# Second attention of a two-layer block by units of four heads, with projections and head outputs kept in DRAM

## The chip, the cores and the metric

The kernel runs on one core of a Trainium2 chip. A core has a matrix engine (PE, TensorE), a vector engine (DVE), an activation engine (ACT), a general engine (POOL) and a sync engine (SP) that only issues transfers; each takes its own instructions in order, and they wait for one another by semaphores. PE writes its results to PSUM, of which this program lays out eight banks of 512 float32 per partition; DVE and ACT read them from there. The metric is the device time of one execution in microseconds, the median over several runs.

## The reference, cut to what matters

Input x is 4 batches of 2048 rows of 256. Everything is float32.

```python
x = L0_attn_x
xn = _layernorm(x)
s = _L0_attn_ref(xn, Wqkv, Wout)          # 16 heads of 16; segments of 512 rows, every 8th row a key
g = _silu(_L0_ffn_ref(xn, ...))           # x rounded to fp8, 256 x 256 product, bias
x = x + s * g
xn = _layernorm(x)
s = _L1_attn_ref(xn, ...)                 # causal attention, 16 heads of 16, rotary q and k
g = _silu(_L1_ffn_ref(xn, ...))           # mixture of 8 experts, 2 per row, capacity 2048 rows each
x = x + s * g

# second attention
q, k, v = projections with bias; q, k = _apply_rope(q, k)
att = softmax(where(causal, q k^T / 4, -inf)); y = att v; return y wo^T + bo
# second feed-forward: logits -> softmax -> top 2 -> place of each row in its expert's 2048 slots
h = relu(disp w1 + b1); out = h w2 + b2   # 256 -> 1024 -> 256 per expert
y = gate-weighted sum of each row's two results
```

The second attention subtracts each row's true maximum, so every score is computed twice: once for the maxima, once for the exponentials.

## The kernel before, in words

*First layer.* Sixteen segments of 512 rows go through a software pipeline that is written as a plan: `segment(g)` enters its steps under a step number (`at(t0 - 20, load)` and so on), and one loop emits them by number. PSUM is split into two pairs for scores (`sc_tile`, two banks each) and four single banks (`mm_tile`). Most SBUF tiles have two buffers. The normalized result x1n goes to `xn_d` in DRAM, x1 to `x1_d`.

*Routing.* After the first layer, softmax of the logits, the two best experts, running counts by doubling (`scan`), and a table `source` of which row sits in which expert slot; the table is built by 128 one-hot pairs that one accumulating matmul (L542) adds up, with `at_row` from DVE (L538). Nothing else runs beside it.

*Second layer.* PSUM is now three pairs (`pair_tile`, L683's scores) and two single banks (`one_tile`). A ring of five blocks holds q, k and v of 512 rows for all 16 heads in SBUF. For each batch there are two stages:

- `maxima(b)`: for each block of 512 queries, each tile of 128 of them and each group of four heads, the scores against each block of 512 keys (L683, four matmuls on the four row groups of the array) into two pairs; DVE takes maxima of a pair (L720). On the diagonal ACT copies the 128 x 128 part (L723), POOL masks it (L731), DVE takes its maximum (L740), and L725 takes the part left of it. The negated maxima are turned (`spread`) and written by DMA into a spare row of q, so that the second scores come out with the maximum subtracted.
- `attend(b)`: for each block, group and tile of 128 keys, scores again, exponential on ACT (L826), on the diagonal a POOL mask (L831), and two items later (`LAG = 2`) the product with v (L846), which sums in one single bank; then `heads_out` and `out_rows` turn, divide and project.

`project` (L619 turns x1n, L626 q and k, L635 v, L652 to L657 the rotation, L666 and L671 the turn into the ring) and `experts` (L915 turns the gathered rows, L926 first product, L930 relu on ACT, L941 second product, L947 bias on DVE) are generators; a yield names a rough cost. `along` walks the main stage and lets side generators catch up with their share: in maxima two experts, in attend the next batch's projections. Beside the last attend runs `finish`, which gathers each row's two expert results and writes the output. The order on PE, DVE, ACT and POOL is that of emission.

Of the kernel before, what the change touches and what calls it, by code (L numbers as in the profile page):

```python
# [18 lines left out]
P = 128  # L19
# [24 lines left out]
def d2_kernel(ctx: ExitStack, tc: tile.TileContext, t: dict):  # L44
# [6 lines left out]
    first = ExitStack()  # L51
    ps_sc = first.enter_context(tc.tile_pool(name="ps_sc", bufs=2, space=PSUM))
    ps_mm = first.enter_context(tc.tile_pool(name="ps_mm", bufs=4, space=PSUM))

    def sc_tile():
        return ps_sc.tile([P, 2, 512], F32, tag="sc", name="sc")

    def mm_tile():
        return ps_mm.tile([P, 512], F32, tag="mm", name="mm")
# [6 lines left out]
    xn_d = dram.tile([B * M + 1, D], F32, tag="xn_d", name="xn_d")  # L66
    s_d = dram.tile([B * M, D], F32, tag="s_d", name="s_d")
# [7 lines left out]
    def rows(d, n):  # L75
# [11 lines left out]
    early = ExitStack()  # L87
    logits = early.enter_context(tc.tile_pool(name="early", bufs=1)).tile(
        [P, NT, E], F32, tag="logits", name="logits"
    )  # L90
# [28 lines left out]
    def transpose2(out, in_):  # L119

        tp = mm_tile()
        for c in range(2):
            nc.tensor.transpose(tp[:, c * P : (c + 1) * P], in_[:, c * P : (c + 1) * P], ident)
        nc.scalar.copy(out, tp[:, : 2 * P].rearrange("p (c t) -> p c t", c=2))

    def silu(pool, zh):

        th = pool.tile([P, D], F32, tag="se", name="se")
        nc.scalar.activation(th, zh, AF.Tanh)
        nc.vector.scalar_tensor_tensor(zh, th, 1.0, zh, ALU.add, ALU.mult)  # L130


    with ExitStack() as l0:
        w0 = l0.enter_context(tc.tile_pool(name="w0", bufs=1))
        p2 = l0.enter_context(tc.tile_pool(name="l0p2", bufs=2))
        small = l0.enter_context(tc.tile_pool(name="l0small", bufs=4))
# [27 lines left out]
        for i in range(3):  # L164
            v_ = w0.tile([P, 8, 2, HD + 1], F32, tag=f"vbd{i}", name=f"vbd{i}")
            nc.vector.tensor_copy(v_[:, :, :, HD], bc(dmask[:, None, :], [P, 8, 2]))
            vbds.append(v_)
# [7 lines left out]
        def at(step, f, *args):  # L175
            plan.setdefault(step, []).append((f, args))

        def segment(g):
# [3 lines left out]
            def load():  # L182
                v["x"] = x = p2.tile([P, SPT, D], F32, tag="x", name="x", bufs=6)
                nc.sync.dma_start(out=x, in_=rows(x_d, g))
# [7 lines left out]
            def norm(tag):  # L192
                v[tag] = xn = p2.tile([P, SPT, D], F32, tag=tag, name=tag)
# [5 lines left out]
            def turn_x(c):  # L199
                if c == 0:  # L200
                    v["xnT"] = p2.tile([P, 2, SEG], F32, tag="xnT", name="xnT")

                    v["xdil"] = p2.tile([P, 2, 2, KN], F32, tag="xdil", name="xdil")
                tp = mm_tile()
                for a in range(SPT):
                    nc.tensor.transpose(
                        tp[:, a * P : (a + 1) * P], v["xn"][:, a, c * P : (c + 1) * P], ident
                    )
                nc.scalar.copy(v["xnT"][:, c, :], tp)
                for u in range(2):  # L210
                    nc.gpsimd.tensor_copy(v["xdil"][:, c, u, :], v["xnT"][:, c, ::DIL])

            def to_fp8(half):


                if half == 0:
                    v["xq"] = xq = p2.tile([P, 2, SEG], F32, tag="xq", name="xq", bufs=3)
# [4 lines left out]
                mag = p2.tile([P, 2, SEG], F32, tag="mag", name="mag")  # L222
# [7 lines left out]
            def q_proj(ec):  # L230
                if ec == 0:
                    v["qT"] = p2.tile([P, 2, SEG], F32, tag="qT", name="qT")
                pq = mm_tile()
                for c in range(2):
                    nc.tensor.matmul(  # L235
                        pq, lhsT=wqkv[:, c, ec * P : (ec + 1) * P], rhs=v["xnT"][:, c, :],
                        start=(c == 0), stop=(c == 1),
                    )
                nc.scalar.mul(v["qT"][:, ec, :], pq, SCALE)

            def k_proj():

                pk = mm_tile()
                for ec in range(2):
                    for c in range(2):
                        nc.tensor.matmul(
                            pk[:, ec * KN : (ec + 1) * KN],
# [3 lines left out]
                v["kbd"] = kbd = p2.tile([P, 2, 2, KN], F32, tag="kbd", name="kbd")  # L251
                for ec in range(2):
                    nc.vector.tensor_tensor(
                        kbd[:, ec, :, :],
                        bc(pk[:, None, ec * KN : (ec + 1) * KN], [P, 2, KN]),
                        bc(hmask[:, :, None], [P, 2, KN]), ALU.mult,
                    )

            def v_proj():
                pv = mm_tile()  # L260
                for c in range(2):
                    nc.tensor.matmul(
                        pv[:, :D], lhsT=v["xdil"][:, c, :, :].rearrange("p u k -> p (u k)"),
                        rhs=wqkv[:, c, 2 * D : 3 * D], start=(c == 0), stop=(c == 1),
                    )
                for u in range(2):
                    nc.vector.tensor_scalar(  # L267
                        vbds[g % 3][:, :, u, 0:HD],
                        pv[:, :D].rearrange("p (j u d) -> p j u d", u=2, d=HD)[:, :, u, :],
# [3 lines left out]
            def scores0(ec):  # L273

                scs = [sc_tile(), sc_tile()]
                for pr in (2, 3, 0, 1):
                    r0 = 32 * pr
# [275 lines left out]

    early.close()
    first.close()

# [573 lines left out]
```

## Time and profile before

| | |
|---|---|
| time, median of 3 runs | 4508.95 us (4506.05 to 4519.44) |
| the profiled execution: its time, its span | 4471.85 us, 4470.1 us |
| busy PE; DVE; ACT; POOL | 4090.9; 2447.8; 1664.1; 851.3 us |
| mean granted PE clock | 0.932 |
| instructions | 57281 |
| written to and read from HBM | 48.24 and 86.03 MB |

A matmul in float32 shows as two records, so "x8" in a timeline is four matmuls. Matmuls are pipelined and their ends are modelled: distances from start to start tell more than busy time. In the group list a line names the engine, the operation, output and inputs, shape, count, busy time and mean, and then the idle time before these instructions with what ended it.

### The profile page before, as it was taken

To read this page: it belongs to the slowest core of one execution; us is meant where nothing else is said; L and a number is where in the kernel's file an instruction comes from. 1 tells how busy PE (TensorE), PEld (TensorE's weight loads), DVE (VectorE), ACT (ScalarE), POOL (GpSimd) and SP (SyncE) were. 2 spreads that over 40 slices of the span, in tenths; PEclk is the share of its full clock that TensorE was granted. 3 is DMA by queue.
4 is the path that set the end of the run, shared out by engine and by line. 5 is a ranking of instruction groups with operands and counts; after the bars stand their busy time and mean duration, and the time that the engine had idled before them with its cause. 6 is when DMAs were issued, how large, how long until landed. Compare 5 with 4: busy or idle time off the path is not lost.

```text
span 4470.1 us, 57281 instructions
## 1 busy us (share of the span) xinstructions
PE 4090.9 (92%) x23560; PEld 1930.8 (43%) x23560; DVE 2447.8 (55%) x3622; ACT 1664.1 (37%) x2548; POOL 851.3 (19%) x1067
## 2 busy tenths in 40 slices
PE   7898966789999998899999998999999989999998
PEld 4666654344443333444433334444333344443333
DVE  7777777667761122777812226777312257775334
ACT  2333310111116664222156652211566522114775
POOL 3333323101100012111100012110000121112444
PEclk8888777699999998899999998999999989999999
DMA  2111000000100001001000001010000010102422
GB/s 77 43 43 43 29 33 25 10 15 24 38 20 6 10 6 41 20 20 39 15 10 6 10 14 46 16 40 18 6 10 6 15 36 20 39 20 74 128 94 75
DMA packets 111240, 138.48 MB, mean 31 GB/s; under 512 B 11393, under 2 KB 99842, under 8 KB 110978
## 3 DMA queue, kind: packets, MB, share of 16 engines
q1 hardware_dynamic: 95922, 98.22, 6.7%
q0 software_dynamic: 12288, 33.57, 2.4%
q8 instruction: 185, 3.03, 0.3%
q10 hardware_dynamic: 2768, 3.02, 0.2%
q14 instruction: 77, 0.63, 0.0%
HBM read 86.03 MB, written 48.24 MB: 30 GB/s over the span
## 4 chain that ended last, share of the span: by engine, by line
PE 79%; DVE 15%; issue 2%; DMA 1%; ACT 1%; POOL 1%; POOLq 0%; ACTq 0%; SPq 0%; DVEq 0%
PE sp L683 29%; PE so L846 11%; PE so L926 10%; PE so L941 9%; DVE mp L720 4%; PE so L626 3%; PE mm L300 2%; PE so L666 2%; PE mm L323 1%; PE so L635 1%; PE so L787 1%; PE sc L278 1%; DVE at_row L538 1%; PE mm L328 1%; PE mm L235 1%
## 5 line engine op out<-in xcount | busy, mean ns | idle before, releaser
L826 ACT ACTIVATE pt<-sp 128x1024 f32<-128x1024 f32 (+3 forms) x1280 | 1076.8, 893 | 577.2 <-PE sp L683 541.6
L720 DVE TENSOR_REDUCE mp<-sp 128x2 f32<-128x1024 f32 x768 | 904.5, 1220 | 317.7 <-PE sp L683 314.9
L683 PE MATMUL sp<-kT,qT 32*128 32x512 f32 (+3 forms) x5120 | 785.1, 615 | 63.9 <-DVE mp L725 25.9
L683 PE MATMUL sp<-qT,kT 32*128 32x512 f32 (+3 forms) x5120 | 783.4, 583 | 13.6 <-ACT pt L826 13.5
L846 PE MATMUL so<-pt,va 128*32 128x512 f32 (+3 forms) x5120 | 604.6, 545 | 10.9 <-POOL pt L831 10.9
L723 ACT COPY dg<-sp 128x256 f32<-128x256 f32 x512 | 165.3, 375 | 962.6 <-PE sp L683 899.1
L926 PE MATMUL so<-xTe,w 128*128 128x512 f32 x1024 | 515.9, 628 | 4.3 <-ACT xTe L918 2.0
L941 PE MATMUL so<-w,hT 128*128 128x256 f32 x2048 | 506.6, 392 | 0.3 <-DVE ot L947 0.3
L731 POOL TENSOR_SCALAR_AFFINE_SELECT dg<-dg 128x512 f32<-128x512 f32 x256 | 163.2, 640 | 1578.7 <-ACT dg L723 1578.6
L683 PEld LDWEIGHTS sp<-kT,qT 32*128 32x128 f32 x5120 | 270.6, 197 | 444.6 <-issue 146.0
L683 PEld LDWEIGHTS sp<-qT,kT 32*128 32x128 f32 x5120 | 282.9, 184 | 407.6 <-issue 254.0
L941 PEld LDWEIGHTS so<-w,hT 128*128 128x128 f32 x2048 | 374.0, 191 | 193.2 <-issue 143.5
L831 POOL TENSOR_SCALAR_AFFINE_SELECT pt<-pt 128x512 f32<-128x512 f32 x256 | 171.7, 672 | 1310.4 <-PE sp L683 677.1
L930 ACT ACTIVATE hT<-so,b 128x512 f32<-128x512 f32 x256 | 176.0, 687 | 572.5 <-PE so L926 572.5
L725 DVE TENSOR_REDUCE mp<-sp 128x2 f32<-128x256 f32 (+2 forms) x384 | 247.5, 687 | 145.2 <-ACT dg L723 144.2
L926 PEld LDWEIGHTS so<-xTe,w 128*128 128x128 f32 x1024 | 178.1, 193 | 283.1 <-issue 199.6
L846 PEld LDWEIGHTS so<-pt,va 128*32 128x32 f32 x5120 | 101.5, 108 | 418.9 <-issue 345.0
L852 DVE COPY avs<-so 128x512 f32<-128x512 f32 x64 | 44.2, 691 | 360.7 <-PE so L846 360.7
L740 DVE TENSOR_REDUCE mp<-dg 128x8 f32<-128x1024 f32 x128 | 155.0, 1211 | 31.5 <-POOL dg L731 31.5
L626 PE MATMUL so<-wqk,xT 128*128 128x512 f32 x256 | 139.9, 672 | 23.8 <-DVE xT L622 9.5
L294 ACT ACTIVATE w<-w 128x1024 f32<-128x1024 f32 x64 | 67.7, 1057 | 241.4 <-DVE w L290 241.4
L300 PE MATMUL mm<-vbd,w 128*128 128x34 f32 x1024 | 128.7, 283 | 21.5 <-DVE vbd L267 21.5
(165 smaller groups left out, 3514.9 us busy)
## 6 DMA issues: line engine op xcount, KB each, us to landing
w<-in_w_dram SPq DMA_DIRECT2D x16, 1024.0 KB, 6.3
eout<-ot SPq DMA_DIRECT2D x32, 512.0 KB, 2.9
x<-in_x_dram SPq DMA_DIRECT2D x16, 512.0 KB, 5.9
x_d<-x SPq DMA_DIRECT2D x16, 512.0 KB, 2.9
xn_d<-x1n SPq DMA_DIRECT2D x16, 512.0 KB, 3.2
xn<-xn_d SPq DMA_DIRECT2D x16, 512.0 KB
fx<-x_d SPq DMA_DIRECT2D x16, 512.0 KB, 5.5
out_dram<-fz SPq DMA_DIRECT2D x16, 512.0 KB, 4.1
```

The source lines that it names most:

```text
L300: nc.tensor.matmul(av[:, j * 34 : (j + 1) * 34], lhsT=v["w", j // 2][:, j % 2, a * P : (a + 1) * P], rhs=vbds[g % 3][:, j, :, :].rearrange ...
L626: nc.tensor.matmul(pqk, lhsT=xT[:, c, :], rhs=wqk[:, c, :], start=(c == 0), stop=(c == 1))
L683: nc.tensor.matmul(pairs[j // 2][:, j % 2, :w], lhsT=lhsT[r0 : r0 + 32], rhs=rhs[r0 : r0 + 32], start=True, stop=True,)
L720: nc.vector.tensor_reduce(mp[:, h0 : h0 + 2, kc], sp, AX.X, ALU.max)
L723: nc.scalar.copy(dg[:, d0 : d0 + 2, :], sp[:, :, r * P : w])
L725: nc.vector.tensor_reduce(mp[:, h0 : h0 + 2, qb + 1], sp[:, :, : r * P], AX.X, ALU.max)
L826: nc.scalar.activation(pt[:, 2 * p : 2 * p + 2, c0:], sp[:, :, : SEG - c0], AF.Exp, scale=SCALE)
L831: nc.gpsimd.affine_select(out=pt[:, :, c0 : c0 + P], in_=pt[:, :, c0 : c0 + P], compare_op=ALU.is_ge, fill=0.0, base=0, pattern=[[0, 4], [ ...
L846: nc.tensor.matmul(av[32 * j : 32 * j + 32, c0:], lhsT=va[:, kt % 4, h0 : h0 + 32], rhs=pt[:, j, c0:], start=(kt == 0), stop=last,)
L926: nc.tensor.matmul(ph, lhsT=w1[:, c, hc * P : (hc + 1) * P], rhs=xT[:, c, :], start=(c == 0), stop=(c == 1),)
L930: nc.scalar.activation(hT[:, hc, :], ph, AF.Relu, bias=b1[:, hc : hc + 1])
L941: nc.tensor.matmul(po[:, u * D : (u + 1) * D], lhsT=hT[:, hc, a * P : (a + 1) * P], rhs=w2[:, hc, :], start=(hc == 0), stop=(hc == 7),)
```

## The change

PSUM has one layout for the whole program: three pairs (`ps_s`), one bank for the sums of attend (`ps_v`), one bank for everything else (`ps_m`, `mm_tile`). The first layer's scores, x, q, value and output tiles use the pairs too, in two halves of a segment instead of four quarters; most of its SBUF tiles have one buffer.

The first layer also stores x1n turned (`xT_ds`). `project` loads that instead of turning, and writes q, k and v to DRAM by batch, q and k by groups of four heads. A unit is one group of four heads of one batch, 16 units in all; `load_unit` brings its q, k and v into one of two sets of SBUF tiles. `attention` runs the first unit's maxima alone and then, for each unit, attend of it beside maxima of the next, one item of each per step, maxima three steps behind (`LEAD`). The values follow their scores by one item instead of two. Head outputs go to DRAM (`y_ds`), and `out_project` loads them back by blocks of 512 rows.

Batch 0's projections run beside the first layer, routing beside the first unit's maxima, the experts after it in all steps up to 13.7 units, `finish` from there. Projection and output pieces are placed between a step's scores and its values, expert pieces after its maxima. Routing's one accumulating matmul became 16 groups of eight, each added on DVE. The second expert product of 512 columns in two halves became one bank of 256 columns per 128 rows.

```diff
-    ps_sc = first.enter_context(tc.tile_pool(name="ps_sc", bufs=2, space=PSUM))
-    ps_mm = first.enter_context(tc.tile_pool(name="ps_mm", bufs=4, space=PSUM))
+    ps_s = ctx.enter_context(tc.tile_pool(name="ps_s", bufs=3, space=PSUM))
+    ps_v = ctx.enter_context(tc.tile_pool(name="ps_v", bufs=1, space=PSUM))
+    ps_m = ctx.enter_context(tc.tile_pool(name="ps_m", bufs=1, space=PSUM))
...
-    ps_s = ctx.enter_context(tc.tile_pool(name="ps_s", bufs=3, space=PSUM))
-    ps_m = ctx.enter_context(tc.tile_pool(name="ps_m", bufs=2, space=PSUM))
...
+    xT_ds = [dram.tile([2, P, M], F32, tag=f"xT_d{b}", name=f"xT_d{b}") for b in range(B)]
+    q_ds = [dram.tile([4, P, M], F32, tag=f"q_d{b}", name=f"q_d{b}") for b in range(B)]
+    k_ds = [dram.tile([4, P, M], F32, tag=f"k_d{b}", name=f"k_d{b}") for b in range(B)]
+    v_ds = [dram.tile([M, H * (HD + 1)], F32, tag=f"v_d{b}", name=f"v_d{b}") for b in range(B)]
+    y_ds = [dram.tile([M, D], F32, tag=f"y_d{b}", name=f"y_d{b}") for b in range(B)]
...
+    def project():
...
+                xT = pp.tile([P, 2, SEG], F32, tag="pxT", name="pxT")
+                nc.sync.dma_start(
+                    out=xT, in_=xT_ds[b][:, :, i * SEG : (i + 1) * SEG].rearrange("c p t -> p c t")
+                )
...
+                            st = pp.tile([P, 4, P], F32, tag="st", name="st", bufs=3)
+                            nc.vector.tensor_copy(st, tp.rearrange("p (g t) -> p g t", g=4))
+                            nc.sync.dma_start(
+                                out=dst[:, :, t0 + u * P : t0 + (u + 1) * P].rearrange(
+                                    "g p t -> p g t"
+                                ),
+                                in_=st,
+                            )
+                            yield 0.55
...
+    def load_unit(n):
+        b, g = n // 4, n % 4
+        held[n] = sets[(sets.index(held[n - 1]) + 1) % len(sets) if n else 0]
+        qT, kT, va = held[n]
+        nc.sync.dma_start(out=qT, in_=q_ds[b][g])
+        nc.sync.dma_start(out=kT, in_=k_ds[b][g])
+        nc.sync.dma_start(
+            out=va[:, :, :VW],
+            in_=v_ds[b][:, g * VW : (g + 1) * VW].rearrange("(i p) c -> p i c", p=P),
+        )
...
+    def attend(n):
...
+                pt = at.tile([P, 4, SEG], F32, tag="pt", name="pt")
+                pairs = scores(
+                    SEG - c0, kT[:, kt * P : (kt + 1) * P], qT[:, qb * SEG + c0 : (qb + 1) * SEG]
+                )
+                for p, sp in enumerate(pairs):
+                    nc.scalar.activation(
+                        pt[:, 2 * p : 2 * p + 2, c0:], sp[:, :, : SEG - c0], AF.Exp, scale=SCALE
+                    )
...
+            yield 1
+            if step:
+                qb, kt = items[step - 1]
+                ppt, c0 = last_pt
+                if kt == 0:
+                    av = ps_v.tile([P, SEG], F32, tag="av", name="av")
...
+    def attention():
+        NU = 4 * B
+        LEAD = 3
...
+        yield from start(0)
+        for _ in maxima(0):
+            yield MX_T, 1
+            turn()
+        for n in range(NU):
+            two = len(sets) == 2 and n + 1 < NU
+            if two:
+                yield from start(n + 1)
+            a = attend(n)
+            m = maxima(n + 1) if two else iter(())
+            a_on, step = True, 0
+            while True:
+                if a_on:
+                    a_on = next(a, None) is not None
+                    if a_on:
+                        yield S_T, 0
+                        next(a)
+                m_on = step < LEAD or next(m, None) is not None
+                if not (a_on or (two and m_on)):
+                    break
+                yield (AV_T if a_on else 0.0) + (MX_T if two and step >= LEAD else 0.0), 1
+                turn()
+                step += 1
...
+    def out_project(pool, done):
...
+            y = pool.tile([P, SPT, D], F32, tag="oy", name="oy")
+            nc.sync.dma_start(out=y, in_=rows(y_ds[b], qb))
...
+            do(t0 - 14, 0, load)
+            do(t0 - 9, 0, stats, "0")
+            do(t0 - 8, 0, norm, "xn")
+            do(t0 - 7, 2.2, turn_x)
+            do(t0 - 4, 3.9, q_proj)
+            do(t0 - 3, 1.6, kv_proj)
...
+                elif went / L0_T > 0.35:
+                    prj.until(PRJ_T * min(1.0, (went / L0_T - 0.35) / 0.55))
...
+            while not rou.over:
+                rou.burst = 3
+                att_step([
+                    (prj, 0, prj_share), (opr, 0, lambda: 1e9),
+                    (rou, 0, lambda: (att.went - t0) * 2.2), (rou, 1, lambda: (att.went - t0) * 2.2),
+                ])
...
+            exp = Side(experts(ep, 0, E), 2)
...
+            last = 13.7 * UNIT_T
+            while not exp.over:
+                att_step([
+                    (prj, 0, prj_share), (opr, 0, lambda: 1e9),
+                    (exp, 1, lambda: EXP_T * (att.went - t0 - 2.0) / (last - t0)),
+                ])
...
+        while not att.over:
+            att_step([
+                (opr, 0, lambda: 1e9),
+                (fin, 1, lambda: NT * (att.went - t0) / (16 * UNIT_T - t0)),
+                (fin, 0, lambda: NT * (att.went - t0) / (16 * UNIT_T - t0)),
+            ])
```

In a pair such as `(exp, 1, ...)` the number is the place in the step: 0 after the scores, 1 after the maxima; the function is the share of the side work that may have been emitted by then, and `Side(..., 2)` lets at most two pieces go at one place.

## The prediction

> **What bounds the kernel now.** I read first the page (PE busy 4090.9 of 4470.1 us), then the busy times by stage, then the timeline inside one stage of each kind, last the chain of waits. The stretches below are my cuts at the stage borders; the columns are stretch, length, busy PE, PE weight loads, DVE, ACT, POOL (instructions), granted PE clock, DMA share, GB/s.
>
> ```profile
> 0.00:616.00 616.00, 526.80 (x2732) 392.66 (x2733) 453.27 (x1031) 187.85 (x397) 223.77 (x264) 0.83 0.15 47
> 616.00:716.00 100.00, 49.75 (x286) 41.98 (x284) 90.47 (x174) 3.40 (x8) 32.93 (x22) 0.77 0.03 11
> 716.00:1340.00 624.00, 551.29 (x2433) 274.90 (x2434) 412.47 (x499) 97.96 (x215) 80.26 (x105) 0.87 0.08 24
> ...
> 1797.00:2254.00 457.00, 438.56 (x2104) 210.50 (x2104) 338.24 (x361) 90.34 (x191) 61.57 (x82) 0.98 0.07 24
> 2254.00:2711.00 457.00, 427.99 (x3034) 155.72 (x3034) 110.27 (x199) 274.46 (x342) 52.89 (x80) 0.96 0.05 15
> ...
> 4083.00:4470.00 387.00, 362.52 (x2706) 121.84 (x2700) 146.14 (x240) 280.71 (x334) 170.91 (x191) 0.98 0.32 103
> ```
>
> First layer 616 us at clock 0.83; routing 100 us, DVE alone; first maxima, with batch 0's projections ahead of them, 624; then pairs of 457 + 457 (maxima beside two experts, attend beside projections); last attend 387. PE leads everywhere but in routing. The timeline of an attend stage without side work (start, length, engine, line, and in brackets the idle time before it):
>
> ```profile
> 2471.91 1.41 PE L683 MATMUL sp<-qT,kT 32*128 32x512 f32 x8
> 2473.24 1.07 PE L846 MATMUL so<-pt,va 128*32 128x512 f32 x8
> 2473.42 1.94 ACT L826 ACTIVATE pt<-sp 128x1024 f32<-128x1024 f32 x2 [0.37 <-PE sp L683]
> 2474.24 1.39 PE L683 MATMUL sp<-qT,kT 32*128 32x512 f32 x8
> ```
>
> One item takes 2.33 us: scores 1.07, values 1.07, and a wait, because three PSUM pairs serve two per item. The same of a maxima stage with an expert piece:
>
> ```profile
> 2911.99 1.14 PE L683 MATMUL sp<-kT,qT 32*128 32x512 f32 x8
> 2913.06 1.98 PE L926 MATMUL so<-xTe,w 128*128 128x512 f32 x4
> 2913.20 2.36 DVE L720 TENSOR_REDUCE mp<-sp 128x2 f32<-128x1024 f32 x2 [0.63 <-PE sp L683]
> ...
> 2914.98 0.93 PE L683 MATMUL sp<-kT,qT 32*128 32x384 f32 x8
> ```
>
> Here PE goes back to back, 1.07 + 1.92. So start-to-start prices are: scores or values 1.07 us at 512 columns (0.86, 0.65, 0.43 at 384, 256, 128), an expert piece L926 1.91, eight of L941 3.5, four transposes 0.6, a projection piece 1.91 (L626) or 1.06 (L635). With these, PE work of one batch is 388 us of 457 in attend and 411 of 457 in maxima: what is to be won in the stages is 10 to 15%, not more.
>
> **What the Trainium skill says.** "TensorE: Matmul & The Clock Gate", Part 1: The HAM clock gate: the array's clock is throttled by default and released by activity over windows of about 3.4 us. The trace agrees: after a PE wait of 1.7 us the piece L926 takes 3.68 instead of 1.98.
>
> ```profile
> 2923.62 0.30 PEld L683 LDWEIGHTS sp<-kT,qT 32*128 32x128 f32 x4 [1.73 <-DVE mp L720]
> 2923.63 0.91 PE L683 MATMUL sp<-kT,qT 32*128 32x384 f32 x4 [1.12 <-DVE mp L720]
> ...
> 2924.47 3.68 PE L926 MATMUL so<-xTe,w 128*128 128x512 f32 x4
> ```
>
> "Perfetto Trace Analysis", Optimizing Tensor Performance, Matmuls: independent matmul groups should rotate through different PSUM banks, so that one is read out while the next runs. Before has four banks for this in the first layer, two after it. "PSUM — Partial Sum Buffer", PSUM bank collisions: two engines must not touch a bank at once, reads included. The group list agrees: the maximum L725 waits for the copy L723 of the same pair.
>
> ```profile
> L725 DVE TENSOR_REDUCE mp<-sp 128x2 f32<-128x256 f32 (+2 forms) x384 | 247.5, 687 | 145.2 <-ACT dg L723 144.2
> ```
>
> **The change part by part.**
>
> *Steps of the second attention.* The built program has the same 640 score, 640 maxima and 640 value groups, all 32 expert blocks, and the 64 transposes L619 less (about 28 us of PE). After the first unit's maxima, which run alone, there are 685 steps: scores (S), a projection piece, values of the item before (V), maxima (M), an expert piece. Three pairs now serve four tiles per step, and the built program gives the same pair to S and M in each step. That is a loop: S 1.07, to ACT 0.2, exponential 1.03, to PE 0.07, M 1.07, to DVE 0.14, maximum 1.22, to PE 0.07 = 4.87 us, against 3.21 us of PE work in S, V, M. A step is at least max(2.37, 2.14 + projection piece) + max(2.5, 1.07 + expert piece); a diagonal maximum adds the copy ahead of it. Behind the waiting M stand the expert piece and the next S on PE, and behind that S the next exponentials: ACT and DVE then idle with it. With L926 that gives 5.35, nearly all PE; without an expert piece 4.87, 1.66 of it idle. Counted over the order of the built program, with narrower tiles at their price:
>
> - 367 steps with S, M and an expert piece: 2293 us, PE work 2144
> - 188 steps with S and M, no expert piece: 870 us, PE work 609
> - 85 steps of scores alone (unit starts, last unit): 261, PE work 237
> - 45 steps of maxima alone (unit ends): 142, PE work 95
>
> Sum 3565 us, PE work 3085. "In every step" doesn't hold: the L941 pieces of 3.5 us are paced to every second step, and the step between pays the loop. 116 us of it are pieces that share a step and wait for the one `mm` bank (after L926: 0.2 + ACT 0.69 + 0.07).
> What is not in this: the clock dropping at unit starts and ends, where PE has one narrow group per 2.4 us; diagonal values, which wait for POOL's 0.67 behind the exponential, with one item of lag instead of two; jitter. The same arithmetic for before's last attend gives 361, measured 387 (7% more); for the other attends 405, measured 457 (13%, half of it from a low clock at the stage change). Part of those causes (ACT of the finish, stage changes) is priced elsewhere, so I take 4%, bounds 1 and 8: **3708 us** (3600 to 3850).
>
> *First unit's maxima beside routing.* DVE does both: maxima (904.5 + 247.5 + 155.0 + 13)/16 = 82, routing 90; 172, plus loads of the first unit (6.3 us for 1 MB) and two or three handoffs: **200 us** (185 to 220). The 100 us of routing are gone for that, and the expert weights' loads are under it.
>
> *First layer with batch 0's projections.* The chain of waits shows its pace:
>
> ```profile
> 162.15 2.27 PE mm L300 x16
> ...
> 271.36 2.28 PE mm L300 x16
> ```
>
> 109.2 us for three segments, 36.4 each, of which PE is busy 32.9 (mostly a slow clock), DVE 28.3. The projections (PE 16 x (1.91 + 1.06 + 2 x 0.6) = 67; DVE 16 x (0.69 + 0.42 + 1.38) + 8 x 4.7 = 77) fall on the last 65%, 10.4 segments: 6.4 us of PE each. Buffers go from two to mostly one, and one `mm` bank carries k/v, turned y, turned x1, logits and every projection piece: its eviction stands on DVE behind `weigh` (2 x 2.44), PE waits there, and the clock is not helped. I take 45 us in those, 38 in the others, 34 lead-in: 34 + 213 + 468 = **715 us** (616, where dense pieces lift the clock and pay for themselves, to 800).
>
> *Costed at nothing.* Loads of a unit (2 x 1 MB at 6.3 us and the values): SP issues them when the last scores of the unit before are out, some 18 us ahead of the first maxima that read them; without that cover 5 us times 16 = 80. Stores of q, k, v, xT: 560 DMA issues instead of 207 on SP, behind no PE wait that I see; PE would wait if `st` (three buffers) filled. Rope chunks (2.35 us of DVE) fit the 2.4 us that DVE has free per step.
>
> *End.* Finish over the last 2.3 units: 16 tanh of 1.06 on ACT ahead of exponentials, +20. Last heads go out and in through DRAM (2.9 to land, 5.5 to load), project, finish: +25.
>
> Sum: 715 + 200 + 3708 + 20 + 25 = 4668 us of span. The profiled execution of before took 4471.85 with a span of 4470.1, the median of the runs is 4508.95, 0.83% more; so 4670 x 1.0083 = **about 4700 us, 4.2% slower**.
>
> **Rivals.**
> *The overlap pays (other side).* Dense pieces in the first layer hold its clock up (32.9 x 0.83/0.95 + 6.4 = 35 us a segment), so 616 stays; attention at 1% over the arithmetic: 616 + 185 + 3601 + 45 = 4447, x 1.0083 = 4485. For it: DVE and ACT are under 60% in every step. Against: one bank instead of four in the first layer. It decides where first layer plus surcharge fall by about 180 us.
> *The clock goes cold.* Steps without expert pieces keep the array at some 52% (3 x 0.84 of 4.87; 0.84 is 1.91 less 1.07, one more matmul of 512 columns); if 15% of the 1045 windows of 3.41 us are at half clock, each costs up to 1.7: 267 instead of the 143 of surcharge, and the units without experts more: about 4830.
> *Unit loads stall PE.* SP's queue is in order, values arrive in pieces of 272 bytes: 16 x 5 = 80 more, about 4780. Against it: the 18 us of lead.
>
> **Chances.** Main case 0.5, overlap pays 0.22, cold clock 0.16, loads 0.12. The likeliest is 4700; its own range 4560 to 4830. The range 4480 to 4920 leaves one in ten on either side. This kernel's runs tell about 0.3% from no change: faster 0.19, same 0.05, slower 0.76.
>
> **What would show it.** Right: steps without an expert piece last 4.9 us, with the first S matmul after a gap waiting for the maximum and M for the exponential; PE busy under 90% in units; units 13 and 14 take about 180 us each, the others 235 to 260; first layer over 680 us with PE waiting for DVE evictions of `mm`. Wrong: a first layer at 620, PE at 95% in the units, or a clock under 0.9 in them.

## The result and the profile after

The changed kernel took 4780.88 us (median of 4 runs, 4768.39 to 4792.22) against 4514.19 (4 runs, 4506.05 to 4523.12) of the kernel before: ratio 1.059, 95% interval 1.0554 to 1.0625. 4700 had been forecast. The profiled execution took 4792.22 us with a span of 4790.4, and this time it is the slowest of its kernel's runs, where that of before was the fastest.

Busy times by stage, cut at the borders that the first maxima, the first scores and the changes of tile set give (columns as in the prediction):

```profile
0.00:905.55 905.55, 648.17 (x3012) 473.98 (x3013) 508.81 (x999) 175.44 (x240) 216.38 (x176) 0.73 0.18 59
905.55:1092.30 186.75, 138.91 (x617) 73.52 (x616) 168.09 (x274) 15.91 (x42) 52.43 (x48) 0.70 0.10 33
...
1337.95:1573.00 235.05, 223.76 (x1333) 98.17 (x1332) 110.85 (x143) 92.90 (x136) 28.74 (x40) 1.00 0.17 52
...
4212.10:4421.20 209.10, 182.30 (x1042) 67.30 (x1042) 125.23 (x162) 84.08 (x121) 72.59 (x84) 0.87 0.31 96
4421.20:4634.90 213.70, 187.97 (x996) 62.19 (x992) 134.71 (x173) 87.05 (x124) 79.18 (x88) 0.80 0.27 84
4634.90:4790.00 155.10, 118.78 (x760) 45.04 (x756) 43.84 (x67) 70.82 (x84) 31.05 (x36) 0.83 0.19 58
```

The first layer with batch 0's projections lasts 905.5 us, at clock 0.73 (616 at 0.83 before, without projections). PE stands idle in 257 us of it, against 89 before. The first unit's maxima beside routing take 186.8. The units follow; one of those with experts and the last three are shown: 235, then 209, 214 and 155 to the end.

What the first layer waits for: PE's waits in four segments without projections and in seven with them (who waits, for whom: us in total, times, the longest).

```profile
PE sp L594 <- DVE xn L120: 43.3, 5, 11.3
PE mm L705 <- DVE y L696: 4.1, 4, 1.0
```

```profile
PE sp L594 <- DVE xn L120: 40.3, 5, 9.7
PE mm L210 <- DVE vst L224: 21.1, 3, 10.5
```

The largest by far is the turning of the normalized x (L594), once a segment; over the whole first layer it comes to 125.5 us. Only the second window shows long waits for the eviction of the one `mm` bank (L210 behind `vst`). From one L625 to the next the segments last 48 us without projections (48.4, 48.6, 46.9 after the start) and 60 with them.

A pair of steps in a unit, the first with a 3.5-us expert piece and the second without one (timeline: start, length, engine, line, instruction):

```profile
3858.43 2.26 PE L291 MATMUL sp<-qTb,kTb 32*128 32x512 f32 x8
...
3859.56 0.30 PEld L291 LDWEIGHTS sp<-qTb,kTb 32*128 32x128 f32 x4 [0.94 <-DVE mp L329]
...
3861.62 1.38 PE L291 MATMUL sp<-kTa,qTa 32*128 32x512 f32 x8
3862.93 3.72 PE L1046 MATMUL mm<-w,hT 128*128 128x256 f32 x16
...
3866.58 1.14 PE L291 MATMUL sp<-qTb,kTb 32*128 32x512 f32 x8
...
3869.84 0.91 PE L291 MATMUL sp<-qTb,kTb 32*128 32x384 f32 x4
```

The scores of the first step start on a free pair and then stand 0.94 us for the pair that a maximum still holds. The profile counts them as 2.26 us of work. Step to step it is 8.15 us with the piece and 3.26 without.

### The profile page after: what moved, and what is told of

The parts are those of the page before. It is cut to its first block, busy times and chain, and to the rows that moved or that the text cites. A ratio compares the mean times of both kernels' runs of the same rounds, so it can differ in the third digit from the quotient of the medians.

```text
span 4790.4 us, 57711 instructions
## 1 busy us (share of the span) xinstructions
PE 4232.2 (88%) x23624; PEld 1997.2 (42%) x23624; DVE 2411.0 (50%) x3477; ACT 1675.5 (35%) x2436; POOL 832.3 (17%) x968
## 4 chain that ended last, share of the span: by engine, by line
PE 46%; DVE 5%; ACT 2%; issue 2%; DMA 1%; POOL 0%; POOLq 0%; ACTq 0%; DVEq 0%; SPq 0%
PE sp L291 19%; PE av L416 8%; PE mm L1033 7%; PE mm L1046 7%; DVE mp L325 2%; PE mm L508 1%; PE mm L210 1%; ACT pt L397 1%; ACT hT L1037 1%; DVE mp L329 1%; PE mm L255 1%; PE mm L220 1%; PE mm L373 1%; PE mm L354 1%; PE mm L1022 0%
## 5 line engine op out<-in xcount | busy, mean ns | idle before, releaser
L1033 PE MATMUL mm<-xTe,w 128*128 128x512 f32 x1024 | 512.9, 624 | 16.5 <-ACT hT L1037 7.0
L1046 PE MATMUL mm<-w,hT 128*128 128x256 f32 x2048 | 485.2, 391 | 4.2 <-DVE oyT L503 1.6
L291 PE MATMUL sp<-qTa,kTa 32*128 32x512 f32 (+3 forms) x2560 | 433.7, 590 | 47.8 <-DVE mp L325 31.7
L291 PE MATMUL sp<-qTb,kTb 32*128 32x512 f32 (+3 forms) x2560 | 426.8, 592 | 53.6 <-DVE mp L325 35.4
L1046 PEld LDWEIGHTS mm<-w,hT 128*128 128x128 f32 x2048 | 385.0, 193 | 139.7 <-issue 75.4
L291 PE MATMUL sp<-kTa,qTa 32*128 32x512 f32 (+3 forms) x2560 | 415.5, 617 | 21.2 <-DVE mp L329 9.8
L291 PE MATMUL sp<-kTb,qTb 32*128 32x512 f32 (+3 forms) x2560 | 392.3, 594 | 3.1 <-DVE mp L325 2.1
L1037 ACT ACTIVATE hT<-mm,b 128x512 f32<-128x512 f32 x256 | 175.9, 687 | 550.3 <-PE mm L1033 546.4
L416 PE MATMUL av<-pt,vab 128*32 128x512 f32 (+3 forms) x2560 | 309.0, 555 | 12.4 <-POOL pt L402 12.2
L416 PE MATMUL av<-pt,vaa 128*32 128x512 f32 (+3 forms) x2560 | 310.3, 558 | 4.1 <-POOL pt L402 3.6
L1033 PEld LDWEIGHTS mm<-xTe,w 128*128 128x128 f32 x1024 | 175.1, 191 | 303.3 <-issue 261.0
```

Of the source, the lines that this page charges most:

```text
L291: nc.tensor.matmul(pairs[j // 2][:, j % 2, :w], lhsT=lhsT[r0 : r0 + 32], rhs=rhs[r0 : r0 + 32], start=True, stop=True,)
L416: nc.tensor.matmul(av[32 * j : 32 * j + 32, c0:], lhsT=va[:, kt, h0 : h0 + 32], rhs=ppt[:, j, c0:], start=(kt == 0), stop=last,)
L1033: nc.tensor.matmul(ph, lhsT=w1[:, c, hc * P : (hc + 1) * P], rhs=xT[:, c, :], start=(c == 0), stop=(c == 1),)
L1037: nc.scalar.activation(hT[:, hc, :], ph, AF.Relu, bias=b1[:, hc : hc + 1])
L1046: nc.tensor.matmul(po[:, :D], lhsT=hT[:, hc, a * P : (a + 1) * P], rhs=w2[:, hc, :], start=(hc == 0), stop=(hc == 7),)
```

## The experiments

All kernels are read by the same three stages, since the edits lie in different ones and the kernel before itself differs by a per cent from chip to chip (medians 4473 to 4523). The stages are those of one profiled execution each. The first layer repeats well: two kernels that leave it alone have 905.4 and 904.9 us against 905.5. Attention, from its first scores to PE's last output product, spreads more: the same code in it lasted 3579 to 3598 us in one group of kernels and 3682 to 3691 in another, so differences below some 20 us are not read there. Segments are the means of the third to sixth and of the eighth to fifteenth distance. The last column is the ratio on record, which is not exactly the quotient of two medians.

| run | segment without, with projections | first layer | first maxima | attention | ratio to before |
|---|---|---|---|---|---|
| changed kernel | 47.3, 59.7 | 905.5 | 186.8 | 3691 | 1.059 |
| norm_early | 50.5, 63.6 | 954.1 | 187.5 | 3683 | 1.079 |
| two_mm_banks | 44.4, 51.4 | 813.1 | 187.3 | 3686 | 1.047 |
| half_pieces | 47.3, 59.8 | 905.4 | 186.8 | 3588 | 1.046 |
| norm_banks_halves | 47.7, 55.6 | 872.1 | 186.6 | 3588 | 1.038 |
| turn_in_mm | 44.3, 52.7 | 820.0 | 186.5 | 3598 | 1.019 |
| turn_in_mm_norm | 47.8, 56.8 | 881.0 | 186.6 | 3598 | 1.033 |
| first_psum_as_before | 45.7, 54.2 | 844.9 | 179.8 | 3579 | 1.022 |
| dve_spread | 38.1, 44.2 | 722.9 | 186.9 | 3579 | 0.9994 |
| dve_spread_turn_mm | 38.8, 45.7 | 735.1 | 188.7 | 3598 | 1.0015 |
| order_alone | 37.8, 52.2 | 802.1 | 185.4 | 3682 | 1.038 |
| order_2 | 37.6, 45.5 | 727.8 | 185.2 | 3598 | 0.9998 |
| loads_twice | 47.2, 59.7 | 904.9 | 186.7 | 3683 | one run, 4784.71 us |

**xn ahead of weigh (norm_early).**

```diff
-            do(t0 - 8, 0, norm, "xn")
+            do(t0 - 9, 0, norm, "xn")
```

> One edit: the normalized x of the next segment (DVE, L120) is emitted right after its statistics, ahead of the two weigh steps of the segment in work, instead of behind them. In the profile of the changed kernel PE stands 8 to 11 us per segment at the turning of x (L594) for this xn, 125 us in the whole first layer, and the segments last 48.3 us without and 60 us with projections beside them. Theory A (the order of work on DVE sets the pace, not the number of mm banks): the segments fall to about 40 and 52 us, the first layer from 905 to about 780 us, the whole to about 4650, ratio to before near 1.030. Theory B (the single mm bank sets the pace, as the prediction has it): the wait only turns up again at the mm evictions, the first layer loses under 40 us, ratio 1.05 or more.

The first layer became 49 us longer; neither theory had foreseen a loss. The waits of four segments and the timeline of one, in this run:

```profile
PE sp L594 <- DVE w L672: 43.8, 4, 13.3
```

```profile
219.66 1.38 DVE L120 TENSOR_SCALAR xn<-x,mean,rstd 128x256 f32<-128x256 f32 x4 [3.33 <-POOL rstd L117]
...
225.99 1.94 PE L594 MATMUL sp<-ident,xn 128*128 128x128 f32 x8 [9.85 <-DVE w L672]
```

xn now waits on DVE for POOL's rstd, which stands behind POOL's part of the rounding, and everything queued behind xn waits too. PE stands at the same place, but for something else: the turned x needs a pair, and all three are held, two by scores that `weigh` has not read. The wait that a profile names is the last of several.

**Two `mm` banks in the first layer (two_mm_banks).** The bank of attend's sums is lent to it; after the first layer there is one `mm` bank again.

```diff
-    ps_v = ctx.enter_context(tc.tile_pool(name="ps_v", bufs=1, space=PSUM))
-    ps_m = ctx.enter_context(tc.tile_pool(name="ps_m", bufs=1, space=PSUM))
+    first = ExitStack()
+    ps_v = None
+    ps_m = first.enter_context(tc.tile_pool(name="ps_m0", bufs=2, space=PSUM))
```

> One edit: in the first layer mm has two PSUM banks (the one that the sums of attend use later is lent to it), after the first layer one again. Theory A (order on DVE): only waits for mm evictions can go, which the profile of the changed kernel puts at some 2.7 us per segment without and 8.8 with projections; the wait of 8 us for xn stays. First layer 30 to 60 us shorter (845 to 875), ratio near 1.049. Theory B (the single bank sets the pace): segments fall to about 40 and 48 us, first layer under 790, ratio 1.03 or less.

92 us less, between the two expectations. The segments gain 2.9 us without and 8.3 with projections, about what the waits for `mm` had added up to; the wait for xn stays at 46.3 us in four segments:

```profile
PE sp L595 <- DVE xn L121: 46.3, 4, 11.9
```

So one bank is a cost of its own, half of the 190 us by which the first layer exceeds its forecast of 715, and not the whole.

**The second expert product in halves (half_pieces).**

```diff
-                po = mm_tile()
-                for hc in range(8):
+                for h in range(2):
+                    po = mm_tile()
+                    for hc in range(4 * h, 4 * h + 4):
...
+                    nc.vector.tensor_tensor(
+                        ot[:, a, :], po[:, :D], ot[:, a, :] if h else b2, ALU.add
                     )
-                nc.vector.tensor_tensor(ot[:, a, :], po[:, :D], b2, ALU.add)
-                yield 3.75
+                    yield 1.875
```

> One edit: the second expert product of a row tile (eight matmuls, 3.5 us) is two pieces of four with a DVE eviction each, so that nearly every step of attention gets an expert piece: by the built program 73 steps with scores and maxima have none, instead of 188. Prediction's term (a step without a piece pays the loop through the shared PSUM pair): the same arithmetic gives 3440 us for the steps in place of 3565, so about 125 us less, units 1 to 12 about 229 us each instead of 240, ratio near 1.031. Rival (the waits in the units come from the one mm bank and its evictions, of which this adds 128): no gain or a loss, within 30 us, ratio 1.052 to 1.066.

Attention went from 3691 to 3588 us, 103 less, with 128 evictions more on DVE; the rival's 30 us are exceeded three times over. Steps of full width with no projection or output piece in them last 5.32 us with an L1033 piece, 5.33 with a half piece and 4.77 without an expert piece (medians), against 5.35 and 4.87 of the prediction's arithmetic.

**The three together (norm_banks_halves).**

> The three edits together: xn ahead of weigh, two mm banks in the first layer, second expert product in halves. If their gains come from different waits they add up: 125 + 45 + 125 = about 295 us less than the changed kernel, 4485, ratio near 0.994. If xn and the mm bank are the same wait seen twice, the first layer gains no more than with the better of the two alone, and the ratio is 1.003 or more; if the halves only move waits, it is 1.02 or more.

The first layer takes 872 us and attention 3588. The expected sum counted xn's move as a gain of 125 us. It is a loss here too: 872 is 59 us above the 813 of two_mm_banks. The gains of the bank and of the halves lie in different stages and stay whole.

**The turned x in `mm` (turn_in_mm), and with xn ahead of weigh (turn_in_mm_norm).** Base: two banks and halves. The second has the step number of norm_early besides.

```diff
-                tp = pair_tile()
                 for c in range(2):
+                    tp = mm_tile()
...
-                nc.scalar.copy(xnT, tp)
+                    nc.scalar.copy(xnT[:, c, :], tp)
```

> Base is the changed kernel with two mm banks in the first layer and the second expert product in halves (813 us of first layer in one run and 3588 of attention in the other, so about 4595 together). One edit on it: the turned x (L594) goes to the two mm banks instead of a pair. In the run with xn ahead of weigh, PE stood at the same place and for as long, but waiting for weigh's last read of a pair (L672): the three pairs are held, two by the scores and one by the values. Theory C (two locks on one door: xn behind weigh on DVE, and the pair held by weigh): with one lock off nothing is gained, first layer 790 to 825, ratio about 1.027. Theory B (single mm bank): the turn takes a bank from the others, first layer 830 or more. A third view, that the pairs alone set the pace: first layer under 740.

> The same, and xn emitted ahead of weigh: both locks off. Theory C: the 8 to 11 us per segment at the turning of x go, about 120 us; first layer 680 to 710, the whole about 4475, ratio near 1.00. If the pace is set by the length of the handoffs between the engines in general (each step of a segment waits for the one before on another engine), the wait goes elsewhere and the first layer stays over 770, ratio 1.02.

The first is at 820 as the theory of two locks says, the second at 881, far from its 680 to 710. PE's waits of the second in four segments:

```profile
PE mm L595 <- DVE xn L121: 31.1, 4, 8.3
PE mm L706 <- ACT xnT L598: 29.7, 4, 7.4
```

So the locks were not off. xn, emitted earlier, still came late, since it stands for POOL's rstd as in norm_early, and the bank was passed on to the next user only after ACT had copied the turned x out of it. The forecast fell, and "over 770" of the other view is right as a number; that the locks don't matter is not shown by this run.

**The first layer's PSUM as before (first_psum_as_before).** Two pairs for scores, four banks for all else; in attention the experts are spread to 14.7 units.

```diff
+    ps_s = first.enter_context(tc.tile_pool(name="ps_s0", bufs=2, space=PSUM))
+    ps_m = first.enter_context(tc.tile_pool(name="ps_m0", bufs=4, space=PSUM))
...
-                pq = pair_tile()
                 for ec in range(2):
+                    pq = mm_tile()
...
-            do(t0 - 8, 0, norm, "xn")
+            do(t0 - 9, 0, norm, "xn")
...
-            last = 13.7 * UNIT_T
+            last = 14.7 * UNIT_T
```

> First layer with the PSUM of the kernel before: two pairs for scores only and four mm banks for all else (turned x, q, k and v, values, outputs, turns, projections), values and outputs cut per 128 rows for that; xn ahead of weigh; SBUF buffers and order as in the changed kernel. Halved expert pieces. Beside this, in a stage that the trace shows apart, the experts are spread to 14.7 units instead of 13.7. Theory C (pairs and banks are the coupling): segments without projections 36 to 39 us as in the kernel before, with them 43 to 47, first layer 640 to 690. If the single SBUF buffers and the order are the coupling: first layer over 730. For the spread: the arithmetic of steps gives nothing (3437 against 3440); if the low clock of the units without experts is what they lose, the last three units take 40 us less than the 566 of the halved pieces. Whole about 4450 with both, ratio 0.995.

845 us, with the very PSUM layout of the kernel before. xn ahead of weigh is in it, which cost 49 to 61 us in the runs above; an estimate from them for the layout alone is some 790, still 70 above the run that follows. PE stands for xn here as well, 28.8 us in four segments. So four banks alone don't bring the segments from 46 us to the 36 of before. The experts' spread gains nothing clear: the last three units take 595 us in place of 566, the units before them together 38 us less, and attention as a whole, 3579 us, lies within the spread of its kind.

**DVE's work spread over the eight steps (dve_spread, dve_spread_turn_mm).** What was left was the order. The change had moved DVE's work as well; these lines of its diff are not in the extract shown:

```diff
-            at(t0 - 5, to_fp8, 0)
-            at(t0 - 4, to_fp8, 1)
...
-                at(t0 + 2 * i, weigh, i)
...
+            do(t0 - 2, 0, to_fp8, 0)
+            do(t0 - 1, 0, to_fp8, 1)
...
+                do(t0 + 2 * (i - i % 2), 1.1 * (i % 2), weigh, i)
```

A segment starts every eight steps. The rounding came to lie next to the statistics, and the four `weigh`, one every second step before, became two pairs. One segment of the changed kernel:

```profile
199.75 1.90 PE L685 MATMUL sp<-vbd,w 128*128 128x34 f32 x8
...
207.82 1.22 DVE L672 TENSOR_TENSOR w<-sp,cm 128x1024 f32<-128x1024 f32 x1
208.96 1.37 DVE L120 TENSOR_SCALAR xn<-x,mean,rstd 128x256 f32<-128x256 f32 x4
...
209.51 2.21 PE L594 MATMUL sp<-ident,xn 128*128 128x128 f32 x8 [7.86 <-DVE xn L120]
```

The gate's product, the rounding, both statistics, two `weigh` and xn follow one another on DVE from 193.4 to 210.3 us without a gap; PE ends its values and stands. The two parts of this segment as stretches:

```profile
192.50:209.00 16.50, 9.15 (x41) 7.48 (x41) 15.04 (x30) 1.77 (x3) 9.97 (x6) 0.50 0.10 33
```

```profile
209.00:240.00 31.00, 27.55 (x136) 20.77 (x140) 12.88 (x26) 9.24 (x14) 3.29 (x4) 0.80 0.16 51
```

In the first DVE is busy 15.0 of 16.5 us and PE 9.2, at half its clock; in the second PE 27.6 of 31 and DVE 12.9. They take turns. The next run, on the base of two banks and halves, changes step numbers only, and gives xq a third buffer; the pairs of `weigh` stay:

```diff
-            do(t0 - 14, 0, load)
-            do(t0 - 9, 0, stats, "0")
-            do(t0 - 8, 0, norm, "xn")
+            do(t0 - 13, 0, load)
+            do(t0 - 11, 0, stats, "0")
+            do(t0 - 9, 0, norm, "xn")
...
-            do(t0 - 2, 0, to_fp8, 0)
-            do(t0 - 1, 0, to_fp8, 1)
+            do(t0 - 5, 0, to_fp8, 0)
+            do(t0 - 4, 0, to_fp8, 1)
...
-            do(t0 + 16, 0, stats, "1")
-            do(t0 + 18, 0, norm, "x1n")
-            do(t0 + 19, 0.6, turn_x1, 0)
-            do(t0 + 20, 0.6, turn_x1, 1)
+            do(t0 + 18, 0, stats, "1")
+            do(t0 + 19, 0, norm, "x1n")
+            do(t0 + 20, 0.6, turn_x1, 0)
+            do(t0 + 21, 0.6, turn_x1, 1)
```

> Base: two mm banks in the first layer and halved expert pieces (first layer 813 us, segments 44.4 us without and 51.4 with projections). Edit: only the step numbers of the first layer's DVE work. In the changed kernel both statistics, the rounding to fp8, xn and two weigh steps lie in three neighbouring steps of the eight; by the trace DVE works there some 16 us in one piece while PE waits, and waits for PE in the rest. Now the rounding is three steps earlier (xq has three buffers for it), the first statistics two earlier, xn one, x1 statistics two later, x1n one later, load one later. Theory E (DVE and PE take turns because DVE's work is in one lump): segments fall to about 38 to 40 and 45 us, first layer 680 to 730, whole near 4490, ratio 0.99 to 1.005. Theory C (the three pairs hold the turned x back): xn is early but PE stands for the pair that weigh frees; first layer 790 or more. If the single SBUF buffers are what couples the segments: 770 or more, with PE or DVE waiting for readers of a tile rather than for data.

> The same, and the turned x goes to the two mm banks instead of a pair. Theory E alone: no more than 15 us away from the run before, either way. Theories C and E together (lump and pair are both needed): first layer 680 to 730 here while the run before stays at 790; ratio 1.00 here.

The first layer lost 90 us, to 722.9, with segments of 38.1 and 44.2. The whole stands at 4504.47 us (12 runs) to 4513.26 of before, ratio 0.9994, interval 0.9982 to 1.0006. Of the 28 us that four segments without projections became shorter against two_mm_banks, 23 are idle time of PE (178.00 less 128.65 in the line below, 150.00 less 123.69 in the second of the two lines under order_2); its busy time fell by 5, so the higher clock is the smaller part of the gain.

```profile
112.00:290.00 178.00, 128.65 (x688) 98.51 (x687) 109.51 (x214) 42.91 (x60) 52.96 (x40) 0.73 0.15 51
```

With the turned x in `mm` the layer is 12 us longer: PE no longer waits there for the pair, but 15.0 us in four segments for the bank that ACT has not emptied. So the pair alone does not set the pace. Nor does the smaller number of SBUF buffers: but for xq's third they are those of the changed kernel, and 38.1 us without projections is within 2 us of the 36.4 that the prediction counted for the kernel before. A segment of the first of these runs:

```profile
211.40 4.04 PE L686 MATMUL sp<-vbd,w 128*128 128x34 f32 x32
...
213.67 3.34 DVE L121 TENSOR_SCALAR xn<-x,mean,rstd 128x256 f32<-128x256 f32 x4 [0.91 <-POOL rstd L118]
...
219.55 1.94 PE L595 MATMUL sp<-ident,xn 128*128 128x128 f32 x8 [4.11 <-DVE w L673]
```

PE's wait at the turned x is 4.1 us instead of 7.9 to 11. Which of the moves matters most, and what share the third xq buffer has, no run tells apart.

**The order without the rest (order_alone).** The changed kernel with these step numbers alone.

> The changed kernel with only the new step numbers of the first layer's DVE work (and the third xq buffer): one mm bank, whole expert pieces. Lump and bank as separate costs: the 92 us that the second bank gave stay lost, the 90 us of the new order are won: first layer 815, ratio near 1.039. If the bank only hurt because DVE came in one lump (its evictions queued behind 16 us of other work): first layer under 770, ratio under 1.03. If the order helps only with a second bank: over 860.

802 us. With it all four combinations of one or two banks and old or new order are there, since halving the expert pieces leaves the first layer as it is: 905, 813, 802 and 723 us. Lump and bank are separate costs, 103 and 92 us of gain alone, 183 together. Without projections the order by itself brings the segment to 37.8; with them one bank still costs 8 us (52.2 to 44.2).

**Two more step numbers (order_2).** On the base of the run with ratio 0.9994.

```diff
-            do(t0 - 9, 0, norm, "xn")
+            do(t0 - 10, 0, norm, "xn")
...
-            do(t0 + 22, 1.0, route)
+            do(t0 + 25, 1.0, route)
```

> The run with two mm banks, halved pieces and the new order (0.9994 of the kernel before), with two more step numbers: xn one step earlier, and the router's logits (L772, 2 us of PE) three steps later, so that they fall between the scores and the values. In that run xn takes 3.34 us instead of 1.38 because it runs beside POOL's gate multiplications, and weigh and the turned x wait behind it, 4.1 us of PE per segment. If that is the cause: segments 38.1 to about 35 us, 44.2 to about 41, first layer 723 to 670 or 690, ratio 0.988 to 0.993. If PE at the clock granted there is the bound (31 of 38 us busy): no gain, within 10 us.

No gain: 727.8 us, ratio 0.9998 (0.9978 to 1.0018). xn did not get away from POOL: the older segment's gate stands in the same step and is emitted first, and xn again takes 3.35 us. The logits did fill the gap, the wait at the turned x fell from 4.1 to 1.3 us; but PE's clock from 112 to 262 us is 0.77 instead of 0.81, and the values beside it take 6.18 us instead of 4.04. That stretch in order_2, and then in the run it is based on:

```profile
112.00:262.00 150.00, 132.31 (x683) 102.91 (x683) 107.08 (x206) 41.78 (x59) 49.96 (x38) 0.77 0.18 60
```

```profile
112.00:262.00 150.00, 123.69 (x681) 95.79 (x681) 106.70 (x206) 41.78 (x59) 49.85 (x37) 0.81 0.18 60
```

Nearly the same instructions are 9 us longer busy. Each line is one execution, on different chips, and that of dve_spread was the fastest of its twelve. No run reached a time clearly under that of the kernel before.

**Loads twice (loads_twice).**

```diff
-        nc.sync.dma_start(out=qT, in_=q_ds[b][g])
...
+        for _ in range(2):
+            nc.sync.dma_start(out=qT, in_=q_ds[b][g])
...
```

(and kT and va likewise)

> The changed kernel with each unit's q, k and v loaded twice, one after the other, in the same place of SP's queue. Rival of the prediction (unit loads stall PE, 80 us): each unit start shows another 5 to 7 us of PE waiting, attention 3691 to about 3780. If the loads are hidden by the 18 us of lead: attention within 15 us of 3691.

From 1092 us to the end the DMA queues moved 226 MB instead of 189, and attention lasted 3683 us. The loads are hidden.

## Why the prediction was right or wrong

Direction and case were right: slower, 4781 within the main case's own range. That the total came within 2% is in part luck: the first layer was 190 us longer than its term, and three other misses, 13, 55 and some 50 us, all fell the other way. By terms of the sum:

- *First layer, 715 (616 to 800).* Measured 905.5. This is the term that failed. Its two paces, 38 us without and 45 with projections, are those of dve_spread (38.1 and 44.2, 723 us in all): of a layer with two `mm` banks and spread DVE work. I had the single bank in the argument but not as a term; measured, it is 92 us. The lump of DVE's work was not in the argument at all, although it stood in the diff: the rounding had moved next to the statistics and to `weigh`. I had compared DVE's sum with the segment (it fits) and not laid its pieces on the eight steps. The order is worth 90 to 103 us. "PE waiting for DVE evictions of `mm`" showed, but behind a larger wait for xn.
- *First maxima beside routing, 200 (185 to 220).* 186.8.
- *Steps, 3708 (3600 to 3850), with 45 for finish and end.* From 1092.3 to the end of the span 3698. By class, the arithmetic and the trace: with scores, maxima and expert piece 2293 and 2438; without a piece 870 and 773; scores alone 261 and 344; maxima alone 142 and 135. The sums, 3565 and 3691, differ by 3.5%, where I had taken 4; but the classes miss by up to 145 us either way and partly cancel. The mechanism, the loop through the shared pair, is borne out by the halved pieces: 103 of the 125 us expected, and 4.77 us for a step without a piece.
- *"Steps without an expert piece last 4.9 us".* 3.95 (median), and the steps with a long piece are longer than computed (7.97 instead of 2.37 + 1.07 + 3.5 = 6.94). As the timeline of the pair of steps reads, all pairs come free during the long piece, the short step runs almost without waiting, and its maximum then holds up the next scores. The sum of two is about right (11.9 against 11.8); which step shows the wait was wrong. With even pieces it is 4.77.
- *"PE busy under 90% in units"; "wrong: PE at 95%".* It is 95% in a unit with experts (223.76 of 235.05), and the sum is right all the same: a bad sign that I chose. Over attention the profile has PE busy for 3445 of 3691 us, while work at the start-to-start prices is 3085, 84%. Part of the difference is waiting hidden in matmuls such as that of 2.26 us above, part the low clock of the last three units. The Trainium skill warns of this ("Perfetto Trace Analysis", Identifying the Most-Contended Engine: matmul busy share does not tell how close a kernel is to its limit). The trace agrees, though the page's reason, that pipelined instructions look smaller, points the other way: here the busy time is larger than the work.
- *Units 13 and 14 about 180.* 209 and 214, at clock 0.87 and 0.80; the others 225 to 254 (235 to 260 forecast). The low clock is here the cost that the rival "the clock goes cold" named, but in these two units and the last (0.83), not in the steps between, where it is 0.99. "A clock under 0.9" was one of the signs of being wrong, and in these three units it came.
- *Factor 1.0083 from profile to median.* It came from one profiled execution of before. For the changed kernel the median is 0.24% below the profiled one, some 50 us of the sum. This, the shorter attention (3698 where 3753 stood) and the first maxima hid most of the 190 us of the first layer.
- *Rivals.* "The overlap pays" fell: the first layer did not stay at 616, its clock went down to 0.73. "Unit loads stall PE" fell by the doubled loads.
- *Two readings that don't enter the sum.* The "PE wait of 1.7 us" ahead of the slow L926 is the idle time of the weight loads; the matmuls themselves stood for 1.12 us, as the line under it says. SP issued 252 DMAs in before's profile, not 207, and 556 in the changed kernel's.

## What to carry to other kernels

In a pipeline whose order is written out by step numbers, lay the pieces of the second engine on the steps, not only its sum against the period: the same DVE work in one lump cost 90 to 103 us of 905 here, with DVE only 56% busy. When a wait is named, ask what would hold the same instruction next: xn moved up alone made the kernel slower, because its own input and the buffer behind it were late too. Even out side work before adding places for it: halving one 3.5-us piece gained 103 us without any work removed.

## What the runs showed of the hardware

DVE and POOL got in each other's way. Group lines of the changed kernel's first layer and of dve_spread's first 700 us, the same instruction of the rounding:

```profile
L609 DVE TENSOR_SCALAR xq<-xq 128x1024 f32<-128x1024 f32 x16 | 24.4, 1523 | 0.5
```

```profile
L610 DVE TENSOR_SCALAR xq<-xq 128x1024 f32<-128x1024 f32 x16 | 11.3, 705 | 0.5
L121 DVE TENSOR_SCALAR xn<-x,mean,rstd 128x256 f32<-128x256 f32 x64 | 47.6, 803 | 13.7 <-POOL rstd L118 13.5
```

It takes 1.52 us beside POOL's gate, 0.71 where POOL stands still; in exchange xn went from 405 to 803 ns, because it came to lie beside the gate. One case in the changed kernel:

```profile
194.21 1.71 POOL L741 TENSOR_TENSOR s<-s,z 128x512 f32<-128x512 f32 x1 [14.23 <-DVE z L740]
194.83 1.65 DVE L609 TENSOR_SCALAR xq<-xq 128x1024 f32<-128x1024 f32 x1
```

DVE's instruction starts inside POOL's and ends 0.56 us after it, as if most of it had run only when POOL was done. The Trainium skill names a cause that fits ("SBUF — State Buffer", SBUF: two separate sides: one pair of ports is shared by DVE and GpSimd as an exclusive lock); the doubled times agree with it, though no run here tests it alone. The spread moved this cost, by an estimate from these means 1.6 us a segment either way (two instructions of the rounding, four of xn), so it is no part of the 90 us.

Filling PE's gaps did not always pay: in order_2's profile the granted clock was 0.77 where dve_spread's was 0.81, and this took back what less waiting at the turned x (7.0 instead of 17.3 us in four segments) had given. Why the clock was lower with fewer waits is open; no run tells it apart.
